# A graph layer's message variances: summed squares of gathered columns and powers on GpSimd in place of gathered reciprocal roots

## Chip, core and metric

The kernel runs on one core of a Trainium2 chip. The metric is the device time of one launch in microseconds (us); three runs of the kernel before took 5981.48, 5981.84 and 5991.1 us, so its time is the median, 5981.84 us.

## What is computed

The input holds 64 graphs of 256 nodes with 128 features and a 0/1 adjacency matrix for each. Four graph layers follow each other; after each, the layer's result is added to its input and the sum is normalised over the 128 features (`_layernorm`). The change concerns layer 3 and the places where a root is taken:

```
m_j = nodes @ W1[:D];  m_i = nodes @ W1[D:]
pre = m_j[:, None, :, :] + m_i[:, :, None, :] + b1            # every pair (i, j)
msg = gelu(_layernorm(pre, g1, be1))                          # over the features
agg = einsum('bijo,bij->bio', msg, adjacency)                 # neighbours only
updated = _layernorm(concat(nodes, agg) @ W2 + b2, g2, be2)
```

Layer 0 takes, over the same neighbours, a maximum of relu(p_i + q_j + b); layer 1 is a message layer with exp-based ELUs and a tanh; layer 2 multiplies twice by D^-1/2 (A + 1) D^-1/2, where D is the row sum. Every `_layernorm` divides by sqrt(variance + 1e-5).

## The kernel before, in words

**Gathering.** Only neighbours matter, and some 12% of the pairs are neighbours. Nodes are ordered by their number of neighbours, and for each half h of the columns (two halves of 128) the k-th neighbour of each node is laid out as a column of a table of 4800 columns: 40 slots of falling width, in seven blocks (RECTS). `hot` is the one-hot matrix of that table (fp8, 128 x 4800 for each half), so a matmul against `hot` gathers the columns of a per-node quantity. The 4800 columns are handled in five tiles, four of 1024 and one of 704 (TILES), for each half: ten tiles for each graph, 640 in all. A block of 512 columns fits one PSUM tile (`bigp`).

**Layer 3 before the change.** With c the (centred) term of the neighbour and d that of the receiving node, a message's pre-activation is c + d. In the stage `third` the kernel makes c in three bf16 parts (`c3`), d of all nodes for both halves as two float32r parts (`dTh`, `dTl`, lines 779 to 783), and the variances of all pairs at once from products c.d, c.c and d.d (lines 761 to 768 and 785 to 796, fp32 matmuls L766, L790, L791), then a root on ScalarE (L796) and a reciprocal on VectorE (L798): `rstd`. The function `scales` then picks, for one tile, the entry of `rstd` that each table column needs: VectorE multiplies `hot` by `rstd` (`v`, L711), TensorE sums over the partitions with a matrix of ones (L720, four column groups), ScalarE copies the sums out of PSUM (L722), and a DMA writes them as one line to DRAM (L724). In the stage `last`, a DMA reads that line back, broadcast to 128 partitions (`rs_s`, L836); TensorE gathers c with three matmuls for each block (L814) and adds d with two identity matmuls for each piece of a block (L820, 13 pieces for each half); VectorE multiplies by `rs_s` on the way out of PSUM (L824); ScalarE takes the Gelu (L825); `fold` sums the slots (L486, L490); a matmul with W2 follows (L865).

**Roots.** A layernorm (`Shared.layernorm`, lines 160 to 180; five for each graph) takes mean and variance on VectorE, a Sqrt on ScalarE (L170), a reciprocal on VectorE (L172) and scales. `layer_2` does the same for the degrees (L267, L269). [...]a change of table is an ACT_TABLE_LOAD.

**Order of the work.** A graph goes through four stages, `first` (layer 0), `second` (layer 1), `third` (layer 2 and the preparations of layer 3) and `last` (layer 3). The 64 graphs are unrolled; stages of four neighbouring graphs are written in turn by `together`, each `yield` being one step and the number beside a stage in STAGES its weight. `scales` runs for four tiles in `third` and for the others in `last`, four tiles ahead of their use (AHEAD). From what is written a list scheduler makes each engine's order at build time; each engine then takes its instructions in that order and waits for each. All DMAs are issued by SyncE (SP), in order. GpSimd has no work in the 64 graphs.

## Time and profile before

| | us |
|---|---|
| median of three runs | 5981.84 |
| the profiled execution | 5987.58 |
| its span, first to last instruction | 5985.6 |
| busy: TensorE (PE), VectorE (DVE), ScalarE (ACT) | 5142.9, 5035.9, 3123.0 |
| weight loads of TensorE (PEld, beside PE) | 3084.2 |
| busy: GpSimd (POOL) | 1.9 |
| mean granted TensorE clock | 0.913 |
| one graph in steady state (from 2999.79 to 3090.87 us) | 91.08 |

In the page's groups a row is one source line on one engine, with the names of the tiles written and read, the number of instructions, their busy time in us, the mean duration of one in ns, and the idle time of the engine just before them with what ended it. "Busy" is the union of the durations; on VectorE neighbouring instructions overlap by some 0.08 us in the records, so that the distance from start to start is shorter than the duration. PE's ends are modelled.

### The profile page before, as it was taken

How to read it: one execution, taken by the hardware profiler on the slowest of the kernel's cores; microseconds unless marked ns; L12 is line 12 of the kernel's file. 1: busy time of each engine (PE TensorE's matmuls, PEld its weight loads, DVE VectorE, ACT ScalarE, POOL GpSimd, SP SyncE). 2: the span in 40 equal slices, each digit the busy share in tenths (PEclk: the TensorE clock that was granted, in tenths of full speed). 3: DMA queues.
4: the chain of work that ended last, by engine and by line, in shares of the span. 5: the costliest groups of instructions: out<-in, count | busy, mean ns of one | idle time of the engine just before them, and what ended most of it. 6: DMA issues, size and time to landing. Idle time of an engine off the chain costs nothing. (4 is left out here: it accounts for less than half of the span.)

```text
span 5985.6 us, 87363 instructions
## 1 busy us (share of the span) xinstructions
PE 5142.9 (86%) x31376; PEld 3084.2 (52%) x31376; DVE 5035.9 (84%) x14015; ACT 3123.0 (52%) x5579; POOL 1.9 (0%) x10
## 2 busy tenths in 40 slices
PE   5888988889889888898898888988988888889887
PEld 2554555555555555555555555555555555555554
DVE  6888888888888888888888888888888888888887
ACT  2455555555555555555555555555555555555555
POOL 0000000000000000000000000000000000000000
PEclk8989989989899899999898998988999989889998
DMA  0112111111111111111211111112111111111112
GB/s 20 54 56 65 57 62 57 65 59 62 58 64 58 59 59 64 63 59 58 63 59 61 58 64 62 59 58 63 60 61 59 62 61 59 58 63 62 59 61 81
DMA packets 155981, 357.97 MB, mean 60 GB/s; under 512 B 16912, under 2 KB 73616, under 8 KB 155536
## 3 DMA queue, kind: packets, MB, share of 16 engines
q1 hardware_dynamic: 155536, 352.29, 18.2%
q8 instruction: 248, 4.06, 0.3%
q14 instruction: 197, 1.61, 0.1%
HBM read 341.38 MB, written 10.85 MB: 59 GB/s over the span
## 5 line engine op out<-in xcount | busy, mean ns | idle before, releaser
L814 PE MATMUL bigp<-hot,c 128*128 128x512 fp8e4 (+1 forms) x3840 | 1019.4, 371 | 128.0 <-DVE lanes L490 115.2
L653 PE MATMUL bigp<-hot,q 128*128 128x512 fp8e4 (+1 forms) x3840 | 1034.9, 370 | 10.2 <-DVE q L497 8.4
L490 DVE TENSOR_TENSOR lanes<-bigp,lanes 128x512 f32<-128x512 f32 (+6 forms) x1536 | 777.9, 506 | 235.3 <-PE bigp L669 159.9
L711 DVE TENSOR_TENSOR v<-hot,rstd 128x1024 f32<-128x1024 fp8e4 (+7 forms) x1280 | 806.1, 651 | 107.5 <-PE mm L720 107.5
L825 ACT ACTIVATE msg<-msg,be,g 128x1024 f32<-128x1024 f32 (+1 forms) x512 | 605.0, 1182 | 339.0 <-DVE msg L824 331.0
L720 PE MATMUL mm<-v,ones 128*32 128x256 f32 (+1 forms) x5120 | 505.9, 443 | 285.6 <-DVE v L711 283.8
L820 PE MATMUL bigp<-dTh,ident_r 128*128 128x512 f32 (+6 forms) x1664 | 721.0, 471 | 0.0
L490 DVE TENSOR_TENSOR sums<-msg,sums 128x1024 f32<-128x1024 f32 (+6 forms) x1024 | 634.0, 619 | 77.8 <-ACT msg L825 66.8
L824 DVE TENSOR_TENSOR msg<-bigp,rs_s 128x512 f32<-128x512 f32 (+1 forms) x1024 | 624.9, 642 | 35.8 <-PE bigp L820 21.9
L722 ACT COPY row<-mm 128x256 f32<-128x256 f32 (+1 forms) x640 | 231.1, 361 | 625.0 <-PE mm L720 615.6
L814 PEld LDWEIGHTS <-c 128*128 128x128 bf16 x3840 | 275.7, 98 | 527.4 <-issue 251.5
L820 PE MATMUL bigp<-dTl,ident_r 128*128 128x512 f32 (+6 forms) x1664 | 529.6, 350 | 0.0
L653 PEld LDWEIGHTS <-q 128*128 128x128 bf16 x3840 | 295.5, 98 | 318.1 <-issue 112.8
L617 DVE TENSOR_SCALAR hot<-rank 128x512 fp8e4<-128x512 bf16 (+5 forms) x1536 | 453.6, 348 | 0.0
L669 PEld LDWEIGHTS <-pick 42*128 42x128 bf16 x2944 | 154.1, 95 | 467.1 <-issue 467.1
L820 PEld LDWEIGHTS bigp<-dTh,ident_r 128*128 128x128 f32 x1664 | 309.3, 190 | 144.4 <-issue 2.9
L865 PE MATMUL mm<-w3u,sums 128*128 128x128 f32 x2048 | 341.4, 318 | 8.5 <-DVE sums L490 8.5
L825 ACT ACT_TABLE_LOAD x259 | 332.3, 1283 | 7.0 <-DVE msg L824 1.5
L720 PEld LDWEIGHTS mm<-v,ones 128*32 128x32 f32 x5120 | 118.6, 118 | 419.5 <-DVE v L711 308.2
L865 PEld LDWEIGHTS mm<-w3u,sums 128*128 128x128 f32 x2048 | 301.0, 223 | 28.5 <-issue 12.2
L820 PEld LDWEIGHTS bigp<-dTl,ident_r 128*128 128x128 f32 x1664 | 294.3, 191 | 23.7 <-issue 0.4
L564 PE MATMUL mm<-perm,nz 128*128 128x256 bf16 x256 | 73.8, 374 | 258.3 <-DVE perm L558 258.3
(242 smaller groups left out, 8546.7 us busy)
## 6 DMA issues: line engine op xcount, KB each, us to landing
rs_s<-line SPq DMA_DIRECT2D x512, 512.0 KB
rs_s<-line SPq DMA_DIRECT2D x128, 352.0 KB
an<-in_adj SPq DMA_DIRECT2D x64, 256.0 KB
x<-in_x SPq DMA_DIRECT2D x64, 128.0 KB
line<-row SPq DMA_DIRECT2D x512, 4.0 KB
out<-o SPq DMA_DIRECT2D x64, 128.0 KB
line<-row SPq DMA_DIRECT2D x128, 2.8 KB
w<-in_L_gnn_W SPq DMA_DIRECT2D x2, 128.0 KB
```

What stands on the lines that cost most here:

```text
L490: nc.vector.tensor_tensor(lanes[:, :k, :w], src[:, i:i + k], lanes[:, :k, :w], op)
L617: nc.vector.tensor_scalar(hot[:, :, at:at + w], rank[:, :, :w], s0 + i + 1.0 - FAR, None, ALU.is_equal, saturate=False)
L653: nc.tensor.matmul(pt[:, :tl], q3[:, i, h], hot[:, h, t0:t0 + tl], start=i == 0, stop=False)
L669: nc.tensor.matmul(o_, l_, r_, start=False, stop=i == len(todo) - 1)
L711: nc.vector.tensor_mul(block(v, m, w, at), block(hot[:, h, tiles[0][0]:], m, w, at), widen(rstd[:, h, :w], m))
L720: nc.tensor.matmul(pr[q * Q:(q + 1) * Q, :n // 4], ones[:, :Q], v4[:, :, q], start=True, stop=True)
L722: nc.scalar.copy(row[:, :n // 4], pr[:, :n // 4])
L814: nc.tensor.matmul(pt[:, :bl], c3[:, i, h], hot[:, h, t0 + b:t0 + b + bl], start=i == 0, stop=False)
L820: nc.tensor.matmul(block(pt[:, :bl], n, w, at), ident_r, widen(q[:, h, :w], n), start=False, stop=q is dTl and i == len(ps) - 1,)
L824: nc.vector.tensor_mul(msg[:, b:b + bl], pt[:, :bl], rs[:, b:b + bl])
L825: nc.scalar.activation(msg[:, :tl], msg[:, :tl], AF.Gelu, bias=be3, scale=g3)
L865: nc.tensor.matmul(pt[:, cols], lanes[:, k, cols], w3u[:, 1], start=k == 0, stop=False)
```

## The change

- `inverse_root` is new: a GpSimd `tensor_tensor` with the operation power, in place, against a constant tile of -0.5. It replaces Sqrt and reciprocal in the layernorms (on 128 x 2 elements; a VectorE instruction that adds epsilon takes the place of the reciprocal) and for the degrees.
- `rstd` for all pairs, `v`, the split of d in `dTh` and `dTl` and the identity matmuls go. `dT` stays as fp32.
- `sums_of` takes the place of `scales` and of the first half of `messages`: the three gathering matmuls for each block, then VectorE adds d on the way out of PSUM (one instruction for each piece) into `pre` (seven buffers of 128 x 1024 fp32), ScalarE squares `pre` into `sq` (one buffer), and the squares are summed over the partitions by the same ones-matmul; ScalarE scales, adds epsilon and writes `row`; a DMA writes the line.
- After every second tile (GROUP) the line of both is read back as 16 elements on each of up to 128 partitions (`vr`), GpSimd takes the power, VectorE multiplies by `fu`, which marks the columns that hold a neighbour, and a DMA writes the result as a new line, which `last` reads back broadcast as before.
- `fu` comes from `fulls`, a DRAM line that `first` writes for each graph (one VectorE comparison of `lack`, and eight DMAs).
- In `last`, VectorE multiplies `pre` by `rs_s` in place, out of SBUF, one instruction for each tile, and the Gelu follows as before.
- STAGES goes from 39, 36, 14, 44 to 34, 34, 14, 44.

```
--- before.py
+++ after.py
@@ -68,6 +68,12 @@
     nc.vector.memset(eps_t, EPS)
     minus1 = consts.tile([P, 1], F32, name="minus1")
     nc.vector.memset(minus1, -1.0)
+    mhalf = consts.tile([P, 16], F32, name="mhalf")
+    nc.vector.memset(mhalf, -0.5)
+
+    def inverse_root(t):
+
+        nc.gpsimd.tensor_tensor(t, t, mhalf[:t.shape[0], :t.free_size()], ALU.pow)
 
...
@@ -165,11 +171,11 @@
             for h in range(H):
                 nc.vector.bn_stats(st[:, h], src[:, h])
                 nc.vector.bn_aggr(mv[:, h], st[:, h])
-            yield
             rs = self.work.tile([P, H], F32, name="rs", bufs=4)
-            nc.scalar.activation(rs, mv[:, :, 1], AF.Sqrt, bias=eps_t)
-            yield
-            nc.vector.reciprocal(rs, rs)
+            nc.vector.tensor_scalar(rs, mv[:, :, 1], EPS, None, ALU.add)
+            yield
+            inverse_root(rs)
+            yield
...
@@ -262,11 +268,10 @@
             nc.vector.tensor_scalar(deg, deg, 1.0, None, ALU.add)
             pos = work.tile([P, H], F32, name="pos")
             nc.vector.tensor_scalar(pos, deg, 0.0, None, ALU.is_gt)
-            nc.vector.tensor_scalar(deg, deg, 1e-30, None, ALU.max)
             dinv = work.tile([P, H], F32, name="dinv")
-            nc.scalar.activation(dinv, deg, AF.Sqrt)
-            yield
-            nc.vector.reciprocal(dinv, dinv)
+            nc.vector.tensor_scalar(dinv, deg, 1e-30, None, ALU.max)
+            inverse_root(dinv)
+            yield
             nc.vector.tensor_mul(dinv, dinv, pos)
             for h in range(H):
                 blk = aT[:, h, h * P:(h + 1) * P]
...
+            full = pair.tile([ROWS, H, N], BF16, name="full")
+            nc.vector.tensor_scalar(full, lack, 0.0, None, ALU.is_equal)
+            s["fulls"] = fulls = dram.tile([H, WIDTH], BF16, name="fulls", bufs=5)
+            for s0, n, w in RECTS:
+                for a, m in ([(s0, n)] if s0 != g_s0 else [(s0, n - 1), (SLOTS - 1, 1)]):
+                    at, r = SLOT_AT[a][0], row_of(a)
+                    nc.sync.dma_start(
+                        fulls[:, at:at + m * w].rearrange("h (s k) -> s h k", k=w), full[r:r + m, :, :w]
+                    )
...
-        CHUNKS = [(h, [t]) for h in range(H) for t in TILES]
+        TODO = [(h, t0, tl) for h in range(H) for t0, tl in TILES]
         AHEAD = 4
-
-        def scales(s, c):
-
-            h, tiles = CHUNKS[c]
-            hot, rstd = s["hot"], s["rstd"]
-            n = sum(tl for t0, tl in tiles)
-            v = big.tile([P, TILE], F32, name="v")
-            for s0, m, w, at in pieces(tiles[0][0], tiles[0][0] + n):
-                nc.vector.tensor_mul(
-                    block(v, m, w, at), block(hot[:, h, tiles[0][0]:], m, w, at), widen(rstd[:, h, :w], m)
-                )
-                yield
-
-            bl = P if n % 512 == 0 else n // 4
-            v4 = v[:, :n].rearrange("p (b q k) -> p b q k", q=4, k=bl)
+        GROUP = 2
+        PIECE = 16
+
+        def sums_of(s, i):
+
+            h, t0, tl = TODO[i]
+            hot, c3, dT = s["hot"], s["c3"], s["dT"]
+            pre = big.tile([P, TILE], F32, name="pre", bufs=7)
+            s["pre", i] = pre
+            for b in range(0, tl, 512):
+                bl = min(512, tl - b)
+                pt = ps_big.tile([P, 512], F32, name="bigp")
+                for k in range(3):
+                    nc.tensor.matmul(
+                        pt[:, :bl], c3[:, k, h], hot[:, h, t0 + b:t0 + b + bl], start=k == 0, stop=k == 2
+                    )
+                for s0, n, w, at in pieces(t0 + b, t0 + b + bl):
+                    nc.vector.tensor_add(
+                        block(pre[:, b:], n, w, at), block(pt, n, w, at), widen(dT[:, h, :w], n)
+                    )
+            sq = big.tile([P, TILE], F32, name="sq", bufs=1)
+            nc.scalar.activation(sq[:, :tl], pre[:, :tl], AF.Square)
+            yield
+
+            bl = P if tl % 512 == 0 else tl // 4
+            v4 = sq[:, :tl].rearrange("p (b q k) -> p b q k", q=4, k=bl)
             pr = psum()
             for q in range(4):
-                nc.tensor.matmul(pr[q * Q:(q + 1) * Q, :n // 4], ones[:, :Q], v4[:, :, q], start=True, stop=True)
+                nc.tensor.matmul(pr[q * Q:(q + 1) * Q, :tl // 4], ones[:, :Q], v4[:, :, q], start=True, stop=True)
             row = big.tile([P, TILE // 4], F32, name="row")
-            nc.scalar.copy(row[:, :n // 4], pr[:, :n // 4])
-            line = dram.tile([1, TILE], F32, name="line")
+            nc.scalar.activation(row[:, :tl // 4], pr[:, :tl // 4], AF.Identity, bias=eps_t, scale=1.0 / P)
+            at = sum(n for _, _, n in TODO[i - i % GROUP:i])
+            if at == 0:
+                s["line"] = dram.tile([1, GROUP * TILE], F32, name="line")
+            line = s["line"]
             nc.sync.dma_start(
-                line[:, :n].rearrange("o (b q k) -> (o q) b k", q=4, k=bl),
-                row.rearrange("(q p) n -> q p n", p=Q)[:, 0, :n // 4].rearrange("q (b k) -> q b k", k=bl),
+                line[:, at:at + tl].rearrange("o (b q k) -> (o q) b k", q=4, k=bl),
+                row.rearrange("(q p) n -> q p n", p=Q)[:, 0, :tl // 4].rearrange("q (b k) -> q b k", k=bl),
             )
-            for t0, tl in tiles:
-                s[h, t0] = line[:, t0 - tiles[0][0]:t0 - tiles[0][0] + tl]
+            yield
+            if i % GROUP < GROUP - 1:
+                return
+
+            n = at + tl
+            rows = n // PIECE
+            first_at = TODO[i - GROUP + 1][0] * WIDTH + TODO[i - GROUP + 1][1]
+            vr = big.tile([P, PIECE], F32, name="vr")
+            nc.sync.dma_start(vr[:rows], line[:, :n].rearrange("o (p k) -> (o p) k", k=PIECE))
+            fu = big.tile([P, PIECE], BF16, name="fu")
+            nc.sync.dma_start(
+                fu[:rows],
+                s["fulls"].rearrange("h w -> (h w)")[first_at:first_at + n].rearrange("(p k) -> p k", k=PIECE),
+            )
+            inverse_root(vr[:rows])
+            nc.vector.tensor_mul(vr[:rows], vr[:rows], fu[:rows])
+            out_line = dram.tile([1, GROUP * TILE], F32, name="scale_line")
+            nc.sync.dma_start(out_line[:, :n].rearrange("o (p k) -> (o p) k", k=PIECE), vr[:rows])
+            at = 0
+            for j in range(i - GROUP + 1, i + 1):
+                s["scale", j] = out_line[:, at:at + TODO[j][2]]
+                at += TODO[j][2]
             yield
 
         def second(g, s):
...
-            c2 = work.tile([P, H], F32, name="c2")
-            for h in range(H):
-                sq = work.tile([P, P], F32, name="sq")
-                nc.scalar.activation(sq, pcv[:, h, 0], AF.Square, scale=0.5 ** 0.5, accum_out=c2[:, h:h + 1])
-            pt = psum()
-            nc.tensor.matmul(pt[:, :N], w3c[:, 0], x3T, start=True, stop=True)
-            cT = work.tile([P, N], F32, name="cT")
-            nc.scalar.copy(cT, pt[:, :N])
...
-            pdv = pd.rearrange("p (h n) -> p h n", h=H)
-            dT = work.tile([P, H, N], F32, name="dT")
-            nc.scalar.activation(dT, pdv, AF.Identity, bias=b3c)
-            dTh = state.tile([P, H, N], F32R, name="dTh")
-            nc.scalar.copy(dTh, dT)
-            dTl = state.tile([P, H, N], F32R, name="dTl")
-            nc.vector.tensor_sub(dTl, dT, dTh.bitcast(F32))
-            d2 = work.tile([P, H, N], F32, name="d2")
-            nc.scalar.activation(d2, pdv, AF.Square, bias=b3c)
-            yield
-            pv = psum()
-            for h in range(H):
-                rows_h, cols = slice(h * P, (h + 1) * P), slice(h * N, (h + 1) * N)
-                nc.tensor.matmul(pv[:, cols], cT[:, rows_h], dT[:, h], start=True, stop=False)
-                nc.tensor.matmul(pv[:, cols], half[:, :P], d2[:, h], start=False, stop=True)
-            yield
-            rstd = state.tile([P, H, N], F32, name="rstd")
-            for h in range(H):
-                nc.scalar.activation(rstd[:, h], pv[:, h * N:(h + 1) * N], AF.Relu, bias=c2[:, h:h + 1])
-            nc.scalar.activation(rstd, rstd, AF.Sqrt, bias=eps_t, scale=2.0 / P)
-            yield
-            nc.vector.reciprocal(rstd, rstd)
-            s.update(x3T=x3T, c3=c3, dTh=dTh, dTl=dTl, rstd=rstd)
-            for c in range(AHEAD):
-                yield from scales(s, c)
+            dT = state.tile([P, H, N], F32, name="dT")
+            nc.scalar.activation(dT, pd.rearrange("p (h n) -> p h n", h=H), AF.Identity, bias=b3c)
+            s.update(x3T=x3T, c3=c3, dT=dT)
+            yield
+            for i in range(AHEAD):
+                yield from sums_of(s, i)
 
         def last(g, s):
 
-            hot, c3, dTh, dTl = (s[k] for k in ("hot", "c3", "dTh", "dTl"))
-
...
-            def messages(h, t0, tl):
-                msg = big.tile([P, TILE], F32, name="msg" if t0 else "sums")
-                rs = scale_of.pop((h, t0))
-                for b in range(0, tl, 512):
-                    bl = min(512, tl - b)
-                    pt = ps_big.tile([P, 512], F32, name="bigp")
-                    for i in range(3):
-                        nc.tensor.matmul(
-                            pt[:, :bl], c3[:, i, h], hot[:, h, t0 + b:t0 + b + bl], start=i == 0, stop=False
-                        )
-                    ps = list(pieces(t0 + b, t0 + b + bl))
-                    for q in (dTh, dTl):
-                        for i, (s0, n, w, at) in enumerate(ps):
-                            nc.tensor.matmul(
-                                block(pt[:, :bl], n, w, at), ident_r, widen(q[:, h, :w], n),
-                                start=False, stop=q is dTl and i == len(ps) - 1,
-                            )
-                    nc.vector.tensor_mul(msg[:, b:b + bl], pt[:, :bl], rs[:, b:b + bl])
-                nc.scalar.activation(msg[:, :tl], msg[:, :tl], AF.Gelu, bias=be3, scale=g3)
-                return msg
-
-            todo = [(h, t0, tl) for h in range(H) for t0, tl in TILES]
-            first_of = {(h, tiles[0][0]): c for c, (h, tiles) in enumerate(CHUNKS)}
             scale_of = {}
 
             def fetch(i):
-                if i < len(todo):
-                    h, t0, tl = todo[i]
-                    scale_of[h, t0] = rs = big.tile([P, TILE], F32, name="rs_s", bufs=3)
-                    nc.sync.dma_start(rs[:, :tl], s.pop((h, t0)).broadcast_to([P, tl]))
+                if i < len(TODO):
+                    scale_of[i] = rs = big.tile([P, TILE], F32, name="rs_s", bufs=3)
+                    nc.sync.dma_start(rs[:, :TODO[i][2]], s.pop(("scale", i)).broadcast_to([P, TODO[i][2]]))
 
             for i in range(2):
                 fetch(i)
             msgs = {}
-            for i in range(len(todo) + 1):
-                if i < len(todo):
-                    c = first_of.get(todo[i][:2], len(CHUNKS)) + AHEAD
-                    if c < len(CHUNKS):
-                        yield from scales(s, c)
-                    msgs[i] = messages(*todo[i])
+            for i in range(len(TODO) + 1):
+                if i < len(TODO):
+                    if i + AHEAD < len(TODO):
+                        yield from sums_of(s, i + AHEAD)
+                    h, t0, tl = TODO[i]
+                    pre, rs = s.pop(("pre", i)), scale_of.pop(i)
+                    nc.vector.tensor_mul(pre[:, :tl], pre[:, :tl], rs[:, :tl])
+                    msgs[i] = msg = pre if t0 else big.tile([P, TILE], F32, name="sums")
+                    nc.scalar.activation(msg[:, :tl], pre[:, :tl], AF.Gelu, bias=be3, scale=g3)
                     fetch(i + 2)
                     yield
                 if i == 0:
                     continue
-                h, t0, tl = todo[i - 1]
+                h, t0, tl = TODO[i - 1]
                 msg = msgs.pop(i - 1)
...
-        STAGES = [(last, 39), (third, 36), (second, 14), (first, 44)]
+        STAGES = [(last, 34), (third, 34), (second, 14), (first, 44)]
```

## The prediction

> **What bounds the kernel now.** First the busy line of the page, then the waits of VectorE and of TensorE, then the groups by form, last the timeline.
>
> ```profile
> PE 5142.9 (86%) x31376; PEld 3084.2 (52%) x31376; DVE 5035.9 (84%) x14015; ACT 3123.0 (52%) x5579; POOL 1.9 (0%) x10
> ```
>
> Two engines stand at 84 to 86% and neither is the sole bound. The waits say what the rest is (engine, line, for whom: us in total, times, longest):
>
> ```profile
> DVE y L248 <- PE mm L244: 175.0, 64, 3.0
> DVE lanes L490 <- PE bigp L669: 159.9, 259, 2.0
> DVE v L711 <- PE mm L720: 107.5, 99, 2.2
> ...
> DVE rstd L798 <- ACT rstd L796: 70.3, 63, 3.4
> ...
> DVE msg L824 <- DMA rs_s<-line: 3.2, 5, 1.9
> ```
> ```profile
> PE mm L720 <- DVE v L711: 283.8, 63, 5.5
> PE mm L564 <- DVE perm L558: 258.3, 64, 4.6
> PE bigp L814 <- DVE lanes L490: 115.2, 122, 1.5
> ```
>
> VectorE's idle time is 5985.6 - 5035.9 = 950 us. Adding its wait rows, some 600 us are for TensorE, 255 for ScalarE, 12 for DMAs. TensorE's 843 us are nearly all for VectorE. Each waits for the other, and a DMA is hardly ever what comes last.
>
> The groups that the change touches (busy us, mean ns | idle before):
>
> ```profile
> L824 DVE TENSOR_TENSOR msg<-bigp,rs_s 128x512 f32<-128x512 f32 x896 | 590.7, 684 | 35.8 <-PE bigp L820 21.9 <-DMA rs_s<-line 3.2 <-DVE dg L542 0.2
> L820 PE MATMUL bigp<-dTh,ident_r 128*128 128x512 f32 x896 | 523.2, 584 | 0.0
> L825 ACT ACTIVATE msg<-msg,be,g 128x1024 f32<-128x1024 f32 x384 | 480.3, 1251 | 313.7 <-DVE msg L824 312.1 <-DVE sums L490 0.6
> L798 DVE RECIPROCAL rstd<-rstd 128x512 f32<-128x512 f32 x64 | 214.6, 3353 | 70.3 <-ACT rstd L796 70.3
> L170 ACT ACT_TABLE_LOAD x132 | 169.4, 1283 | 2.4
> ```
>
> The timeline gives VectorE's true pitch (start, duration):
>
> ```profile
> 3037.32 1.22 DVE L711 TENSOR_TENSOR v<-hot,rstd 128x1024 f32<-128x1024 fp8e4 x1
> 3038.45 0.45 DVE L490 TENSOR_TENSOR sums<-msg,sums 128x284 f32<-128x284 f32 x1
> 3038.82 0.58 DVE L490 TENSOR_TENSOR lanes<-bigp,lanes 128x404 f32<-128x404 f32 x1
> ...
> 3061.11 2.93 DVE L490 TENSOR_TENSOR sums<-msg,sums 128x1024 f32<-128x1024 f32 x4
> ...
> 3089.87 0.95 DVE L824 TENSOR_TENSOR msg<-bigp,rs_s 128x512 f32<-128x512 f32 x2
> ```
>
> 1024 columns take 1.13 us from start to start, 284 take 0.37, and 512 take 0.60 (the 0.68 rows less the overlap): 0.07 us + 1.04 ns a column, from PSUM as from SBUF. The last two rows say how order arises: the folds at 3061.11 are those of tiles 7 and 8, and the product of tile 9, which the code writes before the fold of tile 8, comes 27 us after it. So the scheduler moves work by tens of us, and a chain that is long but foreseen need not stall an engine that waits in order.
>
> **What the Trainium skill says.** "SBUF — State Buffer", section Who interferes with whom: VectorE and GpSimd share a pair of SBUF ports as an exclusive lock. A VectorE instruction in a two-port mode, or with two SBUF inputs against a GpSimd one that reads SBUF, blocks until the other has finished. The trace of before cannot show it: POOL has 10 instructions, all before the graphs. "GPSIMD Engine Reference", sections 3.1 and 7: two-input work takes about 2.6 cycles an element at 1.2 GHz, a dependent fp32 step 4 cycles; no page prices a power. "ScalarE: Activation LUTs", section What ACT_TABLE_LOAD costs: about 1283 ns; the row above agrees, 1283. "DMA: Bandwidth & Descriptors", section Anatomy of one DMA: some 2 us fixed; the trace has SP waiting for a line to land 263 times, at most 2.4 us.
>
> **Part by part.**
>
> *TensorE.* Gone: L820 (721.0 + 529.6), L766 (38.1), L790 (76.5), L791 (76.1): 1441 us busy, so 5143 becomes some 3700. The gathering matmuls and the ones-matmuls stay. TensorE stops being a bound.
>
> *VectorE, by pitch.* Removed: `v`, for each half 3 x 1.13 (1024), then 512, 404, 108, 284, 180, 48, 192 at 0.60, 0.49, 0.18, 0.36, 0.25, 0.12, 0.27 = 5.66 us, by 128 halves 725. Products out of PSUM: 9 x 0.60 + 0.27 = 5.67, by 128 = 725. Reciprocal of `rstd`: 3.27 x 64 = 209. `dTl`: 0.60 x 64 = 39. Together 1698. Added: d on the way out of PSUM, 13 pieces for each half, 7 x 0.60 + 0.49 + 0.18 + 0.36 + 0.25 + 0.12 + 0.27 = 5.87, by 128 = 751. Products out of SBUF, 4 x 1.13 + 0.80 = 5.32, by 128 = 682. The product with `fu`, 320 x 0.12 = 40; `full`, 64 x 0.25 = 16; the epsilon add against the small reciprocal it replaces (0.16 us row), some 0.07 us each at most, 23. Together 1512. Net -186: 5036 becomes 4850.
>
> *ScalarE.* Removed: the small Sqrts with their 132 + 64 + 63 table loads (332 us of loads; about 115 of L170 and L267), and Sqrt, Relu, squares and copies of the `rstd` path, about 265 with L796; some returns to the Gelu table (259 now) may go as well. Added: a Square for each tile; nearest row is the Gelu's 1251 ns for 1024, of which I take 1.2, and 0.9 for 704: 512 x 1.2 + 128 x 0.9 = 730; at the lower end 640. The bias on `row` adds 640 x 0.09 = 58. Sum: 3123 - 712 + 788 = 3200, 54% of the time, not a bound. This work lies beside VectorE's.
>
> *GpSimd.* 5 + 1 powers of 128 x 2 and 5 of 128 x 16 a graph: 384 and 320. Cost of the large one: lower end 0.4 us, like the POOL row of `tail_f` (449 ns for 192 elements, a simple operation); upper end 5 us. Between them an estimate from the page's 4 cycles: if a power is a logarithm and an exponential of together 40 dependent steps, 160 cycles an element, 16 elements take 2.1 us, 2 elements 0.3 plus a start of 0.2. I take 2.0 and 0.5: 320 x 2.0 + 384 x 0.5 = 832 us of POOL. Its own time is hidden behind VectorE; its lock is not. About 45% of VectorE's time is in instructions that contend (the new products 682, `sums` folds 634, `hot` 490, scalar and copy operations on SBUF). A power that starts is soon met by one of these, which then waits for the rest of it: 0 at the lower end, some 0.8 of POOL's time at the upper; I take half, 415 us.
>
> *SP and the new chain.* For each pair of tiles: square 1.2, ones-matmul about 0.8, row 0.4, line 2, `vr` 2, power 2, product 0.1, line 2, broadcast read some 4: 15 us. Behind a waiting product with `fu` stand all later VectorE instructions; behind `vr` and the out line on SP stand the broadcast reads, x, adjacency and `out`. Cover: `pre` has seven buffers, sums run four tiles ahead, three tiles at 8.7 us each give 26 us from the last add to the product. SP now issues 23 DMAs a graph, then 46 at 0.3 to 0.55 us, about 20 of 88 us, with no bandwidth problem (60 GB/s now). If the scheduler's idea of power or DMA is short by 1 us, in-order waits cost 320 x 1 = 320 us, which is inside the range. I charge nothing: the rs_s waits of before are 6 us in total. The mask's eight DMAs fall in `first`, some 80 us before use.
>
> *The sum.* VectorE busy 4850. Idle that remains: of 600 for TensorE a third, as it now has a third more room: 200; of 255 for ScalarE all but the 70 at L798: 185. Lock 415. 4850 + 385 + 415 = 5650 in span; the 2 us outside it, and the profiled execution's standing 6 us above the median, cancel within the rounding. What is late next is VectorE itself.
>
> **Rivals.** *Cheap powers* (lock nearly nil, powers under 1 us): 4850 + 385 + 100 = 5335. For it: 16 elements are little; POOL's simple rows take 0.1 to 0.45 us. Against: a power is no simple operation. *The lock decides* (slower): powers of 4 us and 0.8, of which 0.65 block VectorE: (1280 + 307) x 0.65 = 1030, 4850 + 385 + 1030 = 6265. It becomes slower than before from a VectorE loss of 5986 - 5235 = 750 us on, at a share of one half from 1500 us of POOL's time, that is from powers of about 4 us. For it: the exclusive lock, and VectorE with no slack left. Against: only if a power is that dear and holds its port while it computes. *Nothing comes back* (about 5980): TensorE's gain is taken by waits for `vr`, `row` or `pre` buffers, some 2.3 us for each pair, 330 + 415 us against the 750 of room.
>
> **How the numbers follow.** Forecast (5450 to 5850) 0.43; cheap powers 0.23; nothing comes back 0.06; the lock decides 0.28. Faster by over 0.2% is the first two, 0.66, the third splits into 0.05 for the same and 0.01 beyond it, so slower is 0.29. 0.2%, 12 us, is about what a measurement of this kernel can tell from no change. The range takes in most of the cheap case and half of the lock case: 5290 to 6260. The forecast's own side, all that is faster, is 5290 to 5960.
>
> **What would show it.** TensorE's busy time near 3700 and no L820 rows; VectorE's near 4850 if its records do not contain the lock, and instructions of two SBUF inputs longer than 1.22 us for 1024 columns if they do; POOL's near 830; no table load at L170, L267, L796. Wrong: rows of `pre` products or `sums` folds with means far above 1.22 us (lock), POOL starts over 3 us apart back to back (dear powers), or a VectorE wait for `vr` of more than 100 us in total (chain not covered).

## The result, and the profile after

The changed kernel takes 5989.70 us, the one before 5981.93 us (medians of 20 runs each): a ratio of 1.0012, 95% interval 1.0005 to 1.0019. That is inside the 0.2% that I called no change. The forecast was 5650 us. The profiled execution of the changed kernel took 5983.07 us, its span 5981.0, and one graph still takes 91 us.

The busy line of the page of the kernel after:

```profile
PE 4566.2 (76%) x27408; PEld 2543.8 (43%) x27408; DVE 4764.1 (80%) x13951; ACT 3096.7 (52%) x4924; POOL 1255.0 (21%) x714
```

TensorE, VectorE and ScalarE are all less busy, and the span is the same: work left and idle time came. The waits of VectorE after (engine, line, for whom: us in total, times, longest):

```profile
DVE vr L770 <- POOL vr L76: 743.0, 319, 5.1
DVE kc L543 <- PE mm L535: 90.5, 63, 2.8
DVE io L227 <- PE mm L224: 73.4, 64, 2.8
DVE pre L733 <- PE bigp L729: 59.1, 119, 0.7
```

The waits of before for `lanes` (159.9), `v` (107.5) and `rstd` (70.3) are gone or small. One new row stands above all others: the product with `fu` (L770) waits for the power of the same pair of tiles 319 times of 320, 2.3 us each. VectorE's waits for TensorE fell from 604 us in all to 311, so a slower TensorE (its granted clock was 0.832 here, 0.913 before) is not what holds VectorE up. TensorE's waits for VectorE did not shrink:

```profile
PE mm L297 <- DVE hs L294: 407.8, 67, 7.1
PE mm L567 <- DVE perm L561: 288.1, 64, 4.8
```

The groups on GpSimd after (busy us, mean ns | idle before it):

```profile
L76 POOL TENSOR_TENSOR vr<-vr,mhalf 128x16 f32<-128x16 f32 (+1 forms) x320 | 979.0, 3059 | 2133.5 <-DMA vr<-line 2043.4 <-DVE elu_e L201 41.3 <-DVE sums L493 29.6
L76 POOL TENSOR_TENSOR rs<-rs,mhalf 128x2 f32<-128x2 f32 x320 | 224.3, 701 | 2197.9 <-DVE rs L175 2176.4 <-DVE lanes L493 11.1 <-DVE pre L733 6.5
```

A power of 16 columns takes 3.06 us, of two 0.70. The groups of the scaling products, the new additions and the squares (one row for each shape):

```profile
L840 DVE TENSOR_TENSOR pre<-pre,rs_s 128x1024 f32<-128x1024 f32 x512 | 621.9, 1215 | 18.3 <-DMA rs_s<-scale_line 18.2
L733 DVE TENSOR_TENSOR pre<-bigp,dT 128x512 f32<-128x512 f32 x896 | 604.8, 680 | 36.3 <-PE bigp L729 36.0
L737 ACT ACTIVATE sq<-pre 128x1024 f32<-128x1024 f32 x512 | 540.6, 1056 | 416.3 <-DVE pre L733 236.0 <-DVE lanes L493 177.8
```

The product of two SBUF inputs at L840 takes 1.215 us for 1024 columns, as such instructions did before (the `sums` fold: 1.218 before, 1.217 after). No lock shows in it. The timeline of one chain in the kernel after (start, duration):

```profile
3013.39 0.32 SPq L763 DMA_DIRECT2D vr<-line  x1
...
3015.62 2.90 POOL L76 TENSOR_TENSOR vr<-vr,mhalf 128x16 f32<-128x16 f32 x1 [1.03 <-DMA vr<-line]
3018.56 0.18 DVE L770 TENSOR_TENSOR vr<-vr,fu 128x16 f32<-128x16 f32 x1 [3.23 <-POOL vr L76]
3018.76 0.33 SPq L772 DMA_DIRECT2D scale_line<-vr  x1
3020.21 0.32 SPq L829 DMA_DIRECT2D rs_s<-scale_line  x1
```

VectorE had come to L770 at 3015.33, before the power had even started (at 3015.62, when `vr` landed). It then stood until 3018.56 with all its later work behind it. So an instruction of 0.18 us costs 3.4, and it lands on the busiest engine.

### The profile page after: what moved, and what is told of

Same layout as the page of the kernel before. It is cut to its first block, busy times and chain, and to the rows that moved or that the text cites. A ratio compares the mean times of both kernels' runs of the same rounds, so it can differ in the third digit from the quotient of the medians.

```text
span 5981.0 us, 81999 instructions
## 1 busy us (share of the span) xinstructions
PE 4566.2 (76%) x27408; PEld 2543.8 (43%) x27408; DVE 4764.1 (80%) x13951; ACT 3096.7 (52%) x4924; POOL 1255.0 (21%) x714
## 5 line engine op out<-in xcount | busy, mean ns | idle before, releaser
L76 POOL TENSOR_TENSOR vr<-vr,mhalf 128x16 f32<-128x16 f32 (+1 forms) x320 | 979.0, 3059 | 2133.5 <-DMA vr<-line 2043.4
L737 ACT ACTIVATE sq<-pre 128x1024 f32<-128x1024 f32 (+1 forms) x640 | 641.6, 1003 | 508.5 <-DVE pre L733 328.1
L733 DVE TENSOR_TENSOR pre<-bigp,dT 128x512 f32<-128x512 f32 (+6 forms) x1664 | 853.3, 532 | 59.9 <-PE bigp L729 59.1
L840 DVE TENSOR_TENSOR pre<-pre,rs_s 128x1024 f32<-128x1024 f32 (+1 forms) x640 | 729.8, 1149 | 22.2 <-DMA rs_s<-scale_line 22.0
L76 POOL TENSOR_TENSOR rs<-rs,mhalf 128x2 f32<-128x2 f32 x320 | 224.3, 701 | 2197.9 <-DVE rs L175 2176.4
L770 DVE TENSOR_TENSOR vr<-vr,fu 128x16 f32<-128x16 f32 (+1 forms) x320 | 56.1, 175 | 743.0 <-POOL vr L76 743.0
L842 ACT ACTIVATE pre<-pre,be,g 128x1024 f32<-128x1024 f32 (+1 forms) x512 | 601.8, 1176 | 77.3 <-DVE pre L840 74.6
L493 DVE TENSOR_TENSOR sums<-pre,sums 128x1024 f32<-128x1024 f32 (+6 forms) x1024 | 631.0, 616 | 2.8 <-ACT pre L842 2.4
L744 PE MATMUL mm<-sq,ones 128*32 128x256 f32 (+1 forms) x5120 | 463.5, 439 | 173.6 <-ACT sq L737 170.8
L297 PE MATMUL mm<-aT,hs 128*128 128x256 f32 x512 | 255.9, 653 | 407.8 <-DVE hs L294 407.8
L746 ACT ACTIVATE row<-mm,eps_t 128x256 f32<-128x256 f32 (+1 forms) x640 | 292.7, 457 | 512.3 <-PE mm L744 509.6
L630 DVE TENSOR_SCALAR hot<-rank 128x512 fp8e4<-128x512 bf16 (+5 forms) x1536 | 442.8, 347 | 0.0
L297 PEld LDWEIGHTS mm<-aT,hs 128*128 128x128 f32 x512 | 147.6, 318 | 517.8 <-issue 481.1
```

The source lines that it names most:

```text
L76: nc.gpsimd.tensor_tensor(t, t, mhalf[:t.shape[0], :t.free_size()], ALU.pow)
L297: nc.tensor.matmul(pa[:, :N], hs[:, h], aT[:, h], start=h == 0, stop=h == H - 1)
L493: nc.vector.tensor_tensor(lanes[:, :k, :w], src[:, i:i + k], lanes[:, :k, :w], op)
L630: nc.vector.tensor_scalar(hot[:, :, at:at + w], rank[:, :, :w], s0 + i + 1.0 - FAR, None, ALU.is_equal, saturate=False)
L733: nc.vector.tensor_add(block(pre[:, b:], n, w, at), block(pt, n, w, at), widen(dT[:, h, :w], n))
L737: nc.scalar.activation(sq[:, :tl], pre[:, :tl], AF.Square)
```

## The theories

**In order (A').** The order of the work was made as if the power were short, so the product comes too early in VectorE's order, and all that is queued behind it stands. An order that allows for the power would bring back most of what was forecast. **No slack (B').** The chain from the sums over the line, `vr`, power, product and line to the broadcast has no slack left for 3 us; whoever waits, VectorE for the product or VectorE for `rs_s`, the time is lost. The expectations of e1 and e2 have first forms of these two, A and B. **The lock.** The power holds a port and slows VectorE. **Handing over.** Giving the line to GpSimd and back costs, whatever is computed.

## The experiments

Ratios are to the kernel before, with 95% intervals. Edits are to the changed kernel unless another is named.

**e1: the product on GpSimd.**

```
-            nc.vector.tensor_mul(vr[:rows], vr[:rows], fu[:rows])
+            nc.gpsimd.tensor_mul(vr[:rows], vr[:rows], fu[:rows])
```

> The changed kernel with one edit: the product with the mask fu is done by GpSimd right behind the power, so VectorE no longer has an instruction that waits for the power. Theory A (VectorE's in-order wait of 743 us at that product is what ate the gain): most of it comes back, 5981 - 743 + up to 150 us of waits that come up behind it, 5240 to 5400 us, and VectorE's busy time stays near 4760. Rival B (the chain of DMAs, power and broadcast read is too long for its cover, and the product is only where it shows): VectorE waits for rs_s instead, some 600 us or more, total above 5800. Rival C (GpSimd's power holds the shared SBUF ports, unseen so far because VectorE stood idle during it): with VectorE now running beside the powers, products and folds out of SBUF take well over 1.22 us for 1024 columns, VectorE's busy time rises by 500 us or more, total 5600 to 5950.

Measured: 5920.98 us, 0.9906 (0.9889 to 0.9923). The waits of VectorE in this kernel:

```profile
DVE pre L840 <- DMA rs_s<-scale_line: 426.2, 214, 5.8
DVE pre L733 <- PE bigp L729: 138.7, 124, 1.8
DVE y L331 <- PE mm L871: 97.7, 62, 3.0
```

VectorE no longer waits for the power, and more than half of that wait comes back further on, at the broadcast scales: 426 us where the changed kernel has 22. That speaks for "no slack"; but it is also what "in order" says if the scaling products (L840), too, are placed as for a short power, and e5 decides between the two. SP stands 1642.0 us before the DMA of `scale_line`.

**e2: no root.** The power is replaced by one multiplication on GpSimd; this leaves out the root of layer 3's variances, and nothing else.

```
-            inverse_root(vr[:rows])
+            nc.gpsimd.tensor_mul(vr[:rows], vr[:rows], mhalf[:rows])
```

> The changed kernel with layer 3's power replaced by a GpSimd multiplication with the same constant tile: it leaves out the root of layer 3's message variances. The product with fu stays on VectorE. Theory A (the order was made as if the power were some 2.5 us shorter than it is): the multiplication takes a few tenths of a us, VectorE's wait at the product falls from 743 to under 150 us, total 5300 to 5450. Rival B (chain too long): only 320 x 2.5 us of latency goes, other waits take its place, total above 5700. Rival C (ports): like theory A in total, but then the product on GpSimd with the full power must stay slow.

Measured: 5567.45 us, 0.931 (0.9295 to 0.9326). The operation takes 331 ns in the mean in place of 3059; the wait for `vr` is 15.5 us. The traces of e2 and of the changed kernel have the same instructions in the same order on every engine, SP's DMAs included, so the two differ in the length of this operation alone. The power thus costs 5990 - 5567 = 422 us, and with everything else of the change in place the kernel is 415 us faster than before. And the order of the changed kernel is one that serves for an operation of 0.33 us.

**e3: the small powers alone, in the kernel before; e4: layer 3 alone, with Sqrt and reciprocal for the small roots.**

```
--- kernel before (e3: layernorm; the degrees in the same way)
...
-            nc.scalar.activation(rs, mv[:, :, 1], AF.Sqrt, bias=eps_t)
-            yield
-            nc.vector.reciprocal(rs, rs)
+            nc.vector.tensor_scalar(rs, mv[:, :, 1], EPS, None, ALU.add)
+            yield
+            inverse_root(rs)
+            yield
...
```

> The kernel before with only the powers of 128 x 2 in the layernorms and for the degrees; layer 3's variances as before. Theory A: TensorE and VectorE still hold each other up, 256 or so table loads of 1.28 us go from ScalarE, which is no bound: 5900 to 5990 us, within 1.5% of before. Rival (the small powers carry part of the cost, waits of VectorE for POOL rs): 6000 to 6100.

> The changed kernel with the old roots (Sqrt on ScalarE, reciprocal on VectorE) in the layernorms and for the degrees; layer 3 as changed. Theory A: VectorE's wait at the product with fu stays at 600 us or more and the time stays within 2% of before, 5900 to 6100. Rival (the small powers are what costs): below 5800.

Measured: e3 5887.62 us, 0.9843 (0.9826 to 0.9859); e4 6096.43 us, 1.02 (1.0181 to 1.0218). The two parts have opposite signs: -94 and +114 us. Their product, 1.004, is near the 1.0012 of both together. "No change" is thus a gain and a loss of some 2% each. In e3 ScalarE falls from 3123 to 2670 us, as the small Sqrts and 266 of 650 table loads go.

**e5: layer 3's root on ScalarE and VectorE.**

```
-            inverse_root(vr[:rows])
+            nc.scalar.activation(vr[:rows], vr[:rows], AF.Sqrt)
+            nc.vector.reciprocal(vr[:rows], vr[:rows])
```

> The changed kernel with layer 3's root taken by a Sqrt on ScalarE and a reciprocal on VectorE (128 x 16) in place of GpSimd's power; everything else as changed. It brings back up to 320 pairs of table loads (2.6 us each, some 800 us of ScalarE's time, which has room), and its chain is no shorter than with the power. Theory A' (what costs is that the order was made for a power some 2.5 us shorter than the real one, while ScalarE's times are known to it): VectorE's waits in the product chain fall under 200 us and the total to 5600 to 5850. Rival B' (the length of the chain itself is what costs, whoever takes the root): 5900 to 6100.

Measured: 5692.57 us, 0.952 (0.9504 to 0.9536). ScalarE pays for it, 3874.3 us busy in place of 3096.7: table loads rise from 486 us (379 of them) to 1224 (954). VectorE waits 16.0 us in all for the Sqrt and 57.5 for `rs_s`. This is what A' forecast (5600 to 5850, waits under 200) and not what B' did (5900 to 6100), for the chain has not become shorter. One chain of e5:

```profile
3022.59 0.31 SPq L763 DMA_DIRECT2D vr<-line  x1
...
3024.35 1.28 ACT L769 ACT_TABLE_LOAD   x1
...
3025.64 0.22 ACT L769 ACTIVATE vr<-vr 108x16 f32<-108x16 f32 x1
...
3027.20 0.25 DVE L770 RECIPROCAL vr<-vr 108x16 f32<-108x16 f32 x1
...
3028.52 0.17 DVE L771 TENSOR_TENSOR vr<-vr,fu 108x16 f32<-108x16 f32 x1
```

From the issue of the fetch of `vr` to the end of the product it takes 6.1 us, in the timeline of the changed kernel above 5.35; over all 320 pairs the means are 6.15 and 5.21. What differs is the order. In e5 VectorE comes to the reciprocal 5.26 us after that fetch, in the changed kernel to the product after 2.71 us, long before the power is done. So a longer chain costs 297 us less when VectorE comes to it later. The 780 us more of ScalarE, which has room, are cheaper than the 743 us for which VectorE stands.

**e6, e9, e10: the product later in VectorE's order.** e6 writes the product one tile later in the source; e9 fixes it behind the next tile's last addition, e10 behind the product of the next even tile (`behind` is that instruction).

```
--- e9 and e10 (e6 has the same without `behind` and without the `with` line)
+            s["due"] = (i, n, rows, vr, fu)
+            yield
...
+        def finish(s, behind):
+            i, n, rows, vr, fu = s.pop("due")
+            with tc.issue_after(getattr(behind, "ins", behind)):
                 nc.vector.tensor_mul(vr[:rows], vr[:rows], fu[:rows])
```

> The changed kernel with VectorE's product with fu and the DMA of the scale line written one tile later (behind the next tile's sums); the power itself stays where it was. Theory A' (order made for a short power): by the time VectorE comes to the product the power is done, the wait of 743 us falls under 200, and since the broadcast read is still two tiles ahead of its use, little comes up behind it: 5400 to 5650. Rival B' (the chain has no cover to give): waits for rs_s of 400 us or more come up, 5850 to 6000.

> As the experiment that wrote the product one tile later, but with an order that holds: the product with fu must stand behind the last addition of the next tile on VectorE (issue order only, no added wait). Writing it later alone moved nothing (592.8 us of wait), because the scheduler puts an instruction where it thinks it ready. Theory A' (the product stands too early in VectorE's order, since the order was made for a shorter power): the power gets some 5 to 8 us of other VectorE work in front of the product, the wait falls from 743 to under 250 us, the total to 5450 to 5700. Rival B' (cover): waits for rs_s rise above 300 us, total above 5800.

> The same, with the product still later in the stage last: behind the product of pre and rs_s of the next even tile. Theory A': the wait at the product nearly goes (under 100 us), but the scale line is later by one to three us: 5400 to 5650, close to the experiment before it. Rival B': rs_s waits above 300 us, 5750 or more.

Measured: e6 5874.76 us, 0.9827 (0.9811 to 0.9843); e9 5907.6 us, 0.9882 (0.9865 to 0.9898); e10 5883.45 us, 0.9843 (0.9827 to 0.986). All three are faster than before, and all three miss what A' forecast. VectorE's waits in e10:

```profile
DVE vr L781 <- POOL vr L76: 498.9, 255, 4.5
DVE pre L733 <- PE bigp L729: 118.7, 179, 1.1
DVE pre L850 <- DMA rs_s<-scale_line: 108.5, 159, 6.1
```

The wait for the power falls by a third and the wait for `rs_s` rises from 22 to 109. The instruction can be held back behind another, but the start of the chain moves too: in e10 a DMA of `line` is issued at 3010.35, eight DMAs of `fulls` fill SP's queue up to 3014.41, and only then `vr` is fetched. Nor did the edits move the product far: VectorE comes to it 3.2, 4.4 and 3.6 us after the fetch of `vr` on average (e6, e9, e10), where it came after 2.7 and comes after 5.3 in e5. So these runs show that moving this one instruction by hand is worth 1 to 2%; they do not show what a better order of the whole would give.

**e7: a shorter chain.** Each tile gets its own line of 8 elements on up to 128 partitions, with the product on GpSimd.

```
-        GROUP = 2
-        PIECE = 16
+        GROUP = 1
+        PIECE = 8
...
+            nc.gpsimd.tensor_mul(vr[:rows], vr[:rows], fu[:rows])
```

> The kernel with the product on GpSimd (first experiment), and each tile by itself with 8 elements on each partition, in place of two tiles together with 16: the power is about half as long, twice as many are taken, and a tile no longer waits for its partner; SP issues 15 more DMAs a graph. Theory A': the surplus of the power over its plan halves to some 1.3 us and the chain is shorter by it and by the wait for the partner: waits for rs_s fall from 426 to under 250 us, 5650 to 5850. Rival (SP's queue, with more DMAs that wait in order, is the limit): 5900 to 6050.

Measured: 5706.0 us, 0.9541 (0.9525 to 0.9556). A power of 8 columns takes 1.64 us in the median (2.12 in the mean). There are twice as many, and GpSimd is busy 1868 us in place of 1255, yet the kernel is 284 us faster than the changed one and 215 faster than e1. The busy time of GpSimd is not what costs. As a tile here no longer waits for its partner either, the gain is not that of the shorter power alone.

**e8 and e11: idle powers beside the kernel of e3.** Each adds one power of 128 x 16 for every tile, for which nothing waits; e8's read a constant, e11's read `row`.

```
--- e11
+            nc.gpsimd.tensor_tensor(junk, row[:, :16], half[:, :16], ALU.pow)
```

> The kernel before with the small powers alone (third experiment, 5888 us), and with one more power of 128 x 16 on GpSimd for each tile, on tiles that nothing else reads or writes: 640 x 3 us, some 1950 us of GpSimd beside VectorE's work, which waits for none of it except where a small power queues behind one. If a power held the shared SBUF ports against VectorE: products and folds out of SBUF lengthen or wait, at half the time 900 us more, 6500 to 6900. If it does not: VectorE's durations stay (1.22 us for 1024 columns), and only the small powers come later, by up to 3 us at times: 5890 to 6050.

> The kernel before with the small powers alone, and with one more power of 128 x 16 for each tile, whose result nothing reads, paced this time by reading the tile's row of sums (the unpaced ones were all put at the start and proved nothing on ports). It adds 640 x 2.9 = 1870 us of GpSimd spread over the run, beside VectorE's work. If powers hold the shared SBUF ports against VectorE: instructions out of SBUF wait or lengthen, 6500 us or more. If not: VectorE's durations stay (1.22 us for 1024 columns), and only the small powers queue behind the idle ones, up to 3 us for some of 384: 5900 to 6300.

Measured: e8 7708.41 us, 1.2896 (1.2874 to 1.2917), and it says nothing on the lock: as its powers depend on nothing, they were put in clumps ahead of the small powers, and VectorE waited 1487.9 us for those, once for 915.6 at a stretch. e11, which ties each power to its tile, took 5991.85 us, 1.0018 (1.0011 to 1.0025). Its GpSimd rows:

```profile
L735 POOL TENSOR_TENSOR junk<-row,half 128x16 f32<-128x16 f32 x640 | 2066.6, 3229 | 3140.6 <-ACT row L729 3126.7 <-ACT elu_e L195 3.3
L76 POOL TENSOR_TENSOR rs<-rs,mhalf 128x2 f32<-128x2 f32 x320 | 240.6, 752 | 294.5 <-DVE rs L175 294.4
```

2067 us of powers cost 5992 - 5888 = 104 us, and VectorE's waits for the small roots, which queue behind them on GpSimd, rose by 69 of these (`x` 57 to 77, `o` 37 to 81, `z` 40 to 45 us). Apart from the idle powers e11 has the same instructions in the same order on every engine as e3. Its products and folds of 1024 columns with two SBUF inputs took 1216 ns in the mean where they lay beside a power (257 of them) and 1213 where they did not (383). The lock rival asked for 6500 and falls.

**e12, e13, e17: how the time follows the length of the power.** e12 takes the root in two powers (+0.5, then -1); e13 takes it for 8 of the 16 columns and leaves the others' roots out; e17 is e2 with ten multiplications in place of one and leaves the roots out, as e2 does.

```
--- e12
-            inverse_root(vr[:rows])
+            nc.gpsimd.tensor_tensor(vr[:rows], vr[:rows], up[:rows], ALU.pow)
+            nc.gpsimd.tensor_tensor(vr[:rows], vr[:rows], one_down[:rows], ALU.pow)
--- e13
+            nc.gpsimd.tensor_tensor(vr[:rows, :8], vr[:rows, :8], mhalf[:rows, :8], ALU.pow)
--- e17
+            for _ in range(10):
+                nc.gpsimd.tensor_mul(vr[:rows], vr[:rows], mhalf[:rows])
```

> The changed kernel with the root of layer 3 taken in two powers on GpSimd, +0.5 and then -1, so the chain from the sums to the broadcast is about 3 us longer (6.1 us in place of 3.06) and nothing else changes. Theory (each microsecond of the power is a microsecond of a chain without slack, and without the root 2.7 us less brought 423 us, 155 us for each): 5990 + 3.05 x 155 = 6460 us, range 6300 to 6700, and VectorE's wait for the power near 743 + 3.05 x 320 x 0.5 = 1230 us or more. If every product waited the whole of it: 5990 + 976 = 6960 us. Rival (the price is that of handing the line to GpSimd and back at all, whatever it computes): 5990 to 6060 us.

> The changed kernel with the power taken of 8 of the 16 columns of vr only; it leaves out half the roots of layer 3's variances. The power then takes some 1.6 us (the median of 8 elements in the kernel with pieces of 8). Theory (a chain without slack, straight line between 5567 us at 0.33 us and 5990 us at 3.06 us): 5567 + 1.3 x 155 = 5765 us, range 5700 to 5830. If there is slack up to some length and stalls from there on: 5570 to 5650 us. Rival (handing over costs, not the length): 5930 to 6000 us.

> The kernel without layer 3's root, with ten multiplications by the constant tile on GpSimd in its place in place of one; it leaves out the root of layer 3's variances as that kernel does. Ten of 0.26 us and the gaps make a chain of about 2.7 to 3.3 us, as long as the power, but of ten instructions that the order of the work was planned with, where the power is one. If the length of the chain alone counts: on the line of 0.33, 1.80 and 3.06 us, so 5900 to 6040 us. If it counts that the order was made for a chain much shorter than the real one, so that the product comes too early: the planned order now holds ten instructions, the product is placed later, and the time is 5580 to 5750 us with a wait for vr below 200 us. If the power does something else to the other engines that a multiplication does not: 5580 to 5650 us as well, but with the product waiting in VectorE's order as long as before.

Measured, with e5 beside them. "Length" is from the start of the first operation between `vr` and the product to the end of the last; "comes" and "done" are the times after the issue of the fetch of `vr` at which VectorE comes to the work that waits for the root (in e5 the reciprocal, else the product), and at which the product ends (all means over the 320 pairs, worked out from the starts and ends in the traces).

| kernel | length, us | VectorE comes, us | product done, us | wait for it, us in total | time, us (ratio) |
|---|---|---|---|---|---|
| e2 | 0.33 | 2.50 | 2.73 | 15.5 | 5567.45 (0.931) |
| e13 | 1.80 | 2.69 | 4.04 | 375.4 | 5734.38 (0.9584, 0.9564 to 0.9605) |
| after | 3.06 | 2.71 | 5.21 | 743.0 | 5989.70 (1.0012) |
| e12 | 6.03 | 2.88 | 8.19 | 1642.1 | 7018.6 (1.1733, 1.1701 to 1.1765) |
| e17 | 3.66 | 4.55 | 6.27 | 495.7 | 5879.7 (0.9829, 0.9812 to 0.9845) |
| e5 | 1.30, behind a table load of 1.28 | 5.26 | 6.15 | 16.0 | 5692.57 (0.952) |

The GpSimd groups and the wait in e12:

```profile
L773 POOL TENSOR_TENSOR vr<-vr,up 128x16 f32<-128x16 f32 (+1 forms) x320 | 976.2, 3051 | 2041.7 <-DMA vr<-line 1885.9 <-DVE sums L497 136.0 <-DVE pre L737 9.0
L774 POOL TENSOR_TENSOR vr<-vr,one_down 128x16 f32<-128x16 f32 (+1 forms) x320 | 928.5, 2902 | 25.0
```
```profile
DVE vr L775 <- POOL vr L774: 1642.1, 320, 8.3
```

The price of handing over is nil: without a long operation on GpSimd the wait is 15.5 us. In e2, e13 and the changed kernel the order is the same on every engine, and VectorE comes to the product at nearly the same distance from the fetch however long the root takes. In this order each microsecond of length costs, for each of the 320 pairs, 0.36 us from e2 to e13 (167 us / 320 / 1.47) and 0.63 from e13 to after (255 / 320 / 1.26). From after to e12 it costs 1.08 (1029 / 320 / 2.97), in an order that differs a little. The straight line that I expected for e12 (6460) was too mild: there is cover for part of the first 2 us, and from 3 us on none is left. e13 hit.

e17 hit none of its windows. With the gaps between them its ten multiplications take 3.66 us, longer than the power, so length alone would give more than 5990 us; it took 5880. It is 312 us slower than e2, so a root is not needed for most of the price, and it is no special effect of a power. That it is 110 us faster than after fits its order, in which VectorE comes to the product 1.84 us later. Nine more instructions on GpSimd moved the product by that much, so I estimate that the order allows some 0.2 us for each. What the scheduler takes for a power is not on record.

The table decides between the theories. The time does not follow the moment at which the product is done: e5 and e17 are later than after and faster. It goes with the time for which VectorE stands at the product, and that is set by where the order puts it and by the length of the root together. (e1 has no such wait and stands at the scaling products instead.) "No slack", whatever the order, falls.

**e14, e15: SP relieved.** In e1 and in e7 the DMA of `scale_line` is issued by GpSimd in place of SP.

```
-            nc.sync.dma_start(out_line[:, :n].rearrange("o (p k) -> (o p) k", k=PIECE), vr[:rows])
+            nc.gpsimd.dma_start(out_line[:, :n].rearrange("o (p k) -> (o p) k", k=PIECE), vr[:rows])
```

> The kernel with the product on GpSimd, and the DMA of scale_line issued by GpSimd behind that product in place of SP, where the same DMA kept the whole queue waiting 1642 us. If SP's wait for the product, behind which the broadcast reads of other graphs stand, was what held that kernel at 5921 us: 5650 to 5800 us, the wait of VectorE for rs_s down from 426 us to some 150. If the length of the chain itself holds it: 5860 to 5930 us, rs_s waits of 350 us or more. If a DMA issue is dear for GpSimd: above 5930 us.

> The kernel with pieces of 8 and the product on GpSimd (5706 us), and the DMA of scale_line issued by GpSimd in place of SP. If SP's order still costs there: 5580 to 5680 us, and the fastest so far. If only the chain's length counts: 5690 to 5720 us. If a DMA issue is dear for GpSimd, which then issues 640: above 5740 us.

Measured: e14 6009.34 us, 1.0048 (1.0033 to 1.0063), 88 us slower than e1; e15 5887.86 us, 0.9846 (0.9819 to 0.9872), 182 us slower than e7. SP was not relieved (and the order of VectorE changed as well, so this is no test of one thing alone); its waits in e14:

```profile
SPq L751 <- ACT row L746: 1780.8, 395, 15.0
SPq L765 <- POOL vr L770: 1265.1, 318, 7.7
...
SPq L829 <- DMA scale_line<-vr: 585.1, 318, 8.7
```

The load of `fu` (L765) now waits for the same product, as that frees its buffer, and the broadcast behind it waits longer for the line (585.1 us, 165.4 after). A DMA issue takes GpSimd 0.63 us where it takes SP 0.32. What an SP without that wait would give was not tried.

## Why the prediction was wrong

**The step that failed** is "SP and the new chain": "I charge nothing: the rs_s waits of before are 6 us in total." The wait at the product with `fu` is 743 us, 2.3 us for each pair. The reason given looks at the end of the chain, and there it was right: from the start of the square to the scaling product the kernel has 26.2 us on average, as the "26 us" of cover said, and VectorE waits 22 us in all for `rs_s`. What was left out is the VectorE instruction in the middle of the chain. Both of its parts were written down: "Behind a waiting product with `fu` stand all later VectorE instructions", and "If the scheduler's idea of power or DMA is short by 1 us, in-order waits cost 320 x 1 = 320 us". It was short by some 2.3 us: VectorE comes to the product 2.71 us after the fetch of `vr`, the product is done only after 5.21, and the order is the one of e2, where the operation takes 0.33 us. The prediction took the chain to be foreseen, because the scheduler "moves work by tens of us", and it called the 320 us "inside the range" and put nothing into the sum.

The least likely rival (0.06) has "some 2.3 us for each pair", which is 743 / 320. That figure was worked back from a time that stays the same, so the match in size is luck; what it names, waits for `vr` among others, is right.

**The power** was an estimate (2.0 us for 16 columns, 0.5 for 2); it is 3.06 and 0.70. With 2.0 us the chain would have cost, by the line from e13 to after, 207 us over e2: near 5775. So the error in this figure explains half of the 422, and the other half is a power of the length I did expect, in an order that has no room for it, charged at nothing.

**The lock** (415 us) is not there. The Trainium skill, "SBUF — State Buffer", section Who interferes with whom, says that whichever of VectorE and GpSimd issues first has the shared ports for its whole instruction and the other blocks; the prediction took VectorE's side of that alone. In no run does VectorE show it: 1.215 us for L840 and 1.217 for the folds, as before. In e11 792 `hot` comparisons of 512 columns began while a power ran, and took 413 ns with no idle time before them, where 414 was the mean before the change. GpSimd shows it: in e1 one power took 4.40 us (2.90 alone), and VectorE ran `hot` comparisons of L630 during its first 1.4 us. So in this case it is GpSimd that waits, also where it had begun first.

**The sum, term by term.** VectorE busy 4850 forecast, 4764 measured. Wait for the power 0, 743. Other idle time 385, 5981 - 4764 - 743 = 474. Lock 415, about 0. 5650 against 5981: the error is 743 + 89 - 86 - 415 = 331. The 385 was too low by more than the 89: in e2, where the wait for the power is gone, VectorE's idle time is 5564.6 - 4780.3 = 784 us, with 164 of it for the gather (`pre`) and 143 for `rs_s`. A wait that goes lets others come up.

**TensorE** fell by 577 us, not 1441, to 4566. I had subtracted the sums of the rows that go, but busy time is a union, and L820's matmuls lay beside the gather in the records. Without the records of all the rows that go, the busy time of before is 4612 us, 531 less. The kernel before:

```profile
3009.96 0.82 PE L814 MATMUL bigp<-hot,c 128*128 128x512 fp8e4 x3
3010.43 0.58 PE L820 MATMUL bigp<-dTh,ident_r 128*128 128x512 f32 x1
3010.85 0.40 PE L820 MATMUL bigp<-dTl,ident_r 128*128 128x512 f32 x1
3011.09 0.82 PE L814 MATMUL bigp<-hot,c 128*128 128x512 fp8e4 x3
```

A block takes 1.13 us, though its records sum to 1.80. I took VectorE by its pitch and TensorE not. It did not set the end: at 76% TensorE waits for VectorE (L297, 407.8 us).

**ScalarE** came as worked out: 3200 forecast, 3097 measured; a Square takes 1.06 us, not 1.2. **The broken sign** was among those I listed, "a VectorE wait for `vr` of more than 100 us in total (chain not covered)".

**What was right.** The change frees what it was said to free: VectorE's busy time is within 2% of the sum, and with the root out (e2) the kernel takes 5567, with the root on ScalarE (e5) 5693. That both lie near 5650 is partly chance: without a lock and a wait my sum was 4850 + 385 = 5235, and e2 shows that this was never there. The small powers pay (e3).

**What stays open.** How much of the 422 us an order made for the power's real length would bring back with the power on GpSimd; no run had such an order. The nearest is e5, 125 us above e2, and what these 125 us are (ScalarE's 780 us, the reciprocals, the waits for `rs_s`) was not taken apart. Moving the wait by hand brought back 1 to 2% (e1, e6, e9, e10), a shorter operation 4 to 7% (e7, e13, e2).

The fastest complete kernel here is e5, 5692.57 us, 4.8% below the kernel before.

## What to carry to other kernels

Work that is moved to an idle engine is not paid by that engine's busy time. If an instruction of the busiest engine waits for it in order, it is paid by as much as that instruction comes too early, times how often it runs. So look up two times in the trace: when the busiest engine comes to that instruction, and when what it waits for is ready. An order made at build time can allow for a long chain (e5) or take a long operation for a short one (here). And write the chain down station by station: cover at its end says nothing of an instruction in its middle. Replacing the operation by a trivial one, and doubling it, are two short runs that tell the price at once; a third that takes the same result by another way (e5) tells whether it is the length or the order.

## What was not expected of the hardware

- The power on GpSimd grows with the columns: 0.70 us for 2, 1.66 for 8, 2.95 for 16 (medians, 0.70 a mean), some 0.16 us a column and 0.38 to start; the exponent made no great difference (+0.5: 2902 ns, -1: 2899, -0.5: 2954). A multiplication of 16 columns takes 0.22 to 0.33.
- The granted TensorE clock was lower after the change, 0.832 with TensorE busy 76% of the span, where it was 0.913 at 86% before. It does not follow the busy share alone: it was 0.842 at 67% in e8 and 0.788 at 69% in e12. The gathering matmuls that stay took 385 ns before and 391 after. What sets it was not tested.
- GpSimd, not VectorE, is drawn out when both work: powers of 8 columns in e7 have a median of 1.64 us and a mean of 2.12, and the longest took 7.08. The idle powers of 16 columns took 2.92 us in the mean in e8, in clumps while VectorE stood, and 3.23 in e11, spread over VectorE's work.
